# Layer 0's cross-attention: turning the tokens of groups 1 to 3 through DRAM and VectorE instead of on TensorE

## The chip, the cores and the metric

The kernel runs on one core of one Trainium2 chip. The metric is the device time of one execution, in microseconds; the time of a kernel is the median of several runs. A profile is one further execution, recorded by the hardware profiler. Its span runs from the first instruction to the last; the execution's own time is a little longer.

## The reference, cut to what matters

Two decoder layers work on x, 16 blocks of 128 tokens with 512 features, in float32. Each layer has a self-attention, a cross-attention and a feed-forward part, and each part ends in `x = layernorm(x + part(x))`. The change lies in the first layer's cross-attention:

```python
q_hk = (hidden_q @ Wq.T).reshape(b, s, H, K)
q_big = jnp.einsum('bshk,hkq->bshq', q_hk, w_kc_q)
kv_rope = kv_c * cos[None] + _rotate_half(kv_c) * sin[None]
q_r = jnp.einsum('bshq,hqr->bhsr', q_big, W_qr)
k_r = jnp.einsum('bld,hdr->bhlr', kv_rope, W_kr)
attn = jax.nn.softmax(jnp.einsum('bhsr,bhlr->bhsl', q_r, k_r), axis=-1)
ctx_c = jnp.einsum('bhsl,bld->bhsd', attn, kv_rope)
out = jnp.einsum('bhsd,hkd->bshk', ctx_c, w_kc_kv).reshape(b, s, H * K) @ Wo.T
```

There are 16 heads, 128 context rows of 128 features for each block, and 64 features in a head's scores. Every block attends only to its own context, so the 16 blocks are independent.

## The kernel before, in words

**The stage.** The weights are folded earlier: `wqr` (512 x 1024) takes x straight to all heads' queries, `wkr` takes the rotated context to the keys, and `mT[h]` takes a head's context mean to the output. The 16 blocks go in four groups of four (`NG`, `GB`). For a group, `context` (L572 to L581) puts the features of its contexts and tokens on the partitions, since TensorE contracts over partitions: four transposes of the rotated contexts `kvr` against an identity into one PSUM bank `pk` (L575), a ScalarE copy to `kvT` (L577), and for each block `transpose_x` (L123 to L129): four 128x128 transposes into a bank `tr` (L128) and a ScalarE copy into `xT` (L129).

**Two halves.** A group's heads go in two halves of eight. `project(half)` (L583) runs, for each of four column blocks, the matmuls `pq` (L590) and `pk2` (L593) and the copies to `qT` (ScalarE, L591) and `kT` (VectorE, L594). Then four steps follow, one for each block. The 32 steps of the stage are numbered m = 0 to 31, and a step is written (half, i) below, i being the block in its group.

**One step.** `Heads` makes eight scores on TensorE (L607, two PSUM banks `sc`), the negated maximum on VectorE (L214), eight exponentials with their sums on ScalarE (L219), the reciprocal on VectorE (L225) and the scaling on GpSimd (L226). `turn` transposes the probabilities by way of DRAM: VectorE turns 32x32 blocks into `sq` (L624), SyncE's queue writes `sq` to `away` (L628), and four loads from `away` bring it back as `pT` (L631). One step later `values` multiplies with the context (`av`, L637, copied to `cc` at L642), and one more step later `out` applies `mT` (`po`, L649), VectorE adds it to x (L654), and after the second half `layernorm` follows (VectorE and GpSimd, L111 to L122).

**Work beside it.** Each step from m = 4 on handles two pieces of the feed-forward weights (`pieces`): 24 are summed in absolute value (VectorE, L514), then 16 are cut to three levels (VectorE, L541 and L543); each piece is loaded by SyncE's queue (L508) a step ahead into one of two buffers. `rotate` (L406 to L418) loads a group's contexts into the room `ct` and lets GpSimd compute `kvr` with the room `t2` in four operations. It is traced at step (1, 1) of the group before. Both rooms have one buffer.

**The other way to turn tokens.** `Turn` (L132 to L156) is in the kernel already, for other stages. `send`: ScalarE permutes a block's 512 features into `xp` (L144) and SyncE's queue writes it to DRAM (`turned`, L145). `fetch`: four loads, one for 32 partitions each, in runs of 512 bytes (L151). `back`: one VectorE transpose of 32x32 blocks into `xT` (L154).

**What sets the order.** The framework lays down each engine's queue ahead of time. It takes the instructions that are ready by its own estimate of time, those traced first before the others, and a later one may float ahead when it is ready and its buffer is free. On the chip each queue then runs in that fixed order. `keep_in_program_order` pins an instruction behind the one traced last before it on its engine. A tag with one buffer (`xT`, `kvT`, `ct`, `t2`) is given to the next tile when all users of the one before are done.

Of the kernel before, what the change touches and what calls it, by code (L numbers as in the profile page):

```python
# [12 lines left out]
F32 = mybir.dt.float32  # L13
# [5 lines left out]
P = 128  # L19
NB = 16  # L20
D = 512
KC = D // P
# [24 lines left out]
def decoder_kernel(ctx: ExitStack, tc: tile.TileContext, a: dict, out: bass.AP):  # L47
# [25 lines left out]
    def bank(tag, shape, name):  # L73
        return psum.pool.tile(shape, F32, tag=tag, name=name, bufs=psum.banks[tag])
# [45 lines left out]
    def layernorm(b, engine=nc.vector):  # L120
        mean, rstd = statistics(b)
        engine.tensor_scalar(x[b], x[b], mean, rstd, ALU.subtract, ALU.mult)  # L122

    def transpose_x(xT, b, at):

        tr = bank("mm", [P, KC, P], "tr")
        for k in range(KC):
            nc.tensor.transpose(tr[:, k, :], x[b][:, k * P : (k + 1) * P], ident)  # L128
        nc.scalar.copy(xT[:, :, at : at + P], tr)  # L129
# [159 lines left out]
    GB = 4  # L289
    TG = GB * P  # L290
    NG = NB // GB
# [10 lines left out]
    def fold(pool, i, raw, take):  # L302

        cT = pool.tile([P, P], F32, tag="cT", name="cT")
        ch = pool.tile([P, 2, R], F32, tag="ch", name="ch")

        def inner():
            pc = bank("mm", [P, P], "pc")
            for q in range(3):
                for j in range(2):  # L310
                    nc.tensor.matmul(
                        pc[j * R : (j + 1) * R], lhsT=raw[:, j, D + DCQ + q * R : D + DCQ + (q + 1) * R],
                        rhs=raw[:, j, D + q * P : D + (q + 1) * P], start=(q == 0), stop=(q == 2),
                    )
            nc.vector.tensor_copy(cT, pc)

        def turned():
            pc = bank("mm", [P, P], "pcT")
            nc.tensor.transpose(pc, cT, ident)
            nc.vector.tensor_copy(ch.rearrange("p j r -> p (j r)"), pc)  # L320

        def behind(j):
            o = D + DCQ + 3 * R
            pm = bank("mm", [P, D], "pm")
            nc.tensor.matmul(pm, lhsT=raw[:, j, o : o + DC], rhs=raw[:, j, o + DC : o + DC + D], start=True, stop=True)
            take(mT[2 * i + j], pm)

        def outer():
            pg = bank("mm", [P, KC, 2, R], "pg")
            for k in range(KC):  # L330
                for j in range(2):
                    nc.tensor.matmul(
                        pg[:, k, j, :], lhsT=raw[:, j, k * P : (k + 1) * P], rhs=ch[:, j, :], start=True, stop=True
                    )
            nc.vector.tensor_copy(wqr[:, :, i * P : (i + 1) * P], pg.rearrange("p k j r -> p k (j r)"))

        return [(0.8, inner), (0.86, lambda: behind(0)), (0.2, turned), (0.86, lambda: behind(1)), (1.9, outer)]

    with tc.tile_pool(name="p1", bufs=1) as p1:
# [67 lines left out]
        def rotate(g, ct, kvr, t2):  # L407

            blocks = slice(g * GB, (g + 1) * GB)
            nc.sync.dma_start(ct, a["ctx"][blocks].rearrange("b l d -> l b d"))  # L410

            def turn():
                nc.gpsimd.tensor_tensor(t2[:, :, 0:hd], ct[:, :, hd:DC], bc(s2[:, 0:hd], GB), ALU.mult)
                nc.gpsimd.tensor_tensor(t2[:, :, hd:DC], ct[:, :, 0:hd], bc(s2[:, hd:DC], GB), ALU.mult)
                nc.gpsimd.tensor_tensor(kvr, ct, bc(c2, GB), ALU.mult)
                nc.gpsimd.tensor_tensor(kvr, kvr, t2, ALU.add)

            return turn  # L418
# [128 lines left out]
    with tc.tile_pool(name="p2", bufs=1, reuse_waits="tile") as p2:  # L547
# [8 lines left out]
        def pieces():  # L556

            tern.limits()
            while loaded:
                (n, q, run), raw = loaded.pop(0)  # L560
                run(n, q, raw)
            for _ in range(2):
                if todo:
                    loaded.append((todo[0], tern.load(*todo[0][:2], p2)))
                    todo.pop(0)
# [3 lines left out]
        def room(name):  # L569
            return p2.tile([P, GB, DC], F32, tag=name, name=name)  # L570

        def context(g, kvr):  # L572
            pk = bank("mm", [P, GB, P], "pk")
            for i in range(GB):
                nc.tensor.transpose(pk[:, i, :], kvr[:, i, :], ident)  # L575
            kvT = p2.tile([P, TG], F32, tag="kvT", name="kvT")
            nc.scalar.copy(kvT, pk.rearrange("p b l -> p (b l)"))  # L577
            xT = p2.tile([P, KC, TG], F32, tag="xT", name="xT")
            for i in range(GB):
                transpose_x(xT, g * GB + i, i * P)  # L580
            return xT, kvT  # L581

        def project(xT, kvT, half):  # L583
            qT = p2.tile([P, 4, TG], F32, tag="qT", name="qT")
            kT = p2.tile([P, 4, TG], F32, tag="kT", name="kT")
            for c in range(4):
                cols = slice((4 * half + c) * P, (4 * half + c + 1) * P)
                pq = bank("mm", [P, TG], "pq")
                for k in range(KC):
                    nc.tensor.matmul(pq, lhsT=wqr[:, k, cols], rhs=xT[:, k, :], start=(k == 0), stop=(k == KC - 1))  # L590
                nc.scalar.copy(qT[:, c, :], pq)  # L591
                pk2 = bank("mm", [P, TG], "pk2")
                nc.tensor.matmul(pk2, lhsT=wkr[:, cols], rhs=kvT, start=True, stop=True)  # L593
                nc.vector.tensor_copy(kT[:, c, :], pk2)  # L594
            return qT, kT
# [3 lines left out]
        class Heads:  # L599
# [44 lines left out]
            def out(self, par):  # L644
# [8 lines left out]
                if par == 1:  # L653
                    nc.vector.tensor_tensor(x[self.b], x[self.b], self.po, ALU.add)  # L654
                    if self.half == 1:
                        layernorm(self.b)

        kvr = kvr0
        late = []
        for i in range(LATE, H // 2):  # L660
            raw = pre.tile([P, 2, RAW], F32, tag="pre", name=f"raw{i}")
            nc.sync.dma_start(raw, a["l0x_raw"][i].rearrange("p (h n) -> p h n", h=2))
            late += fold(p2, i, raw, nc.vector.tensor_copy)
        held = {}
        steps = [(g, half, i) for g in range(NG) for half in range(2) for i in range(GB)]
        for m in range(len(steps) + 2):
            if m < len(steps):
                g, half, i = steps[m]
                if i == 0:
                    if half == 0:  # L670
                        kv, (xT, kvT) = kvr, context(g, kvr)
                    qT, kT = project(xT, kvT, half)
                held[m] = Heads(g * GB + i, half, qT, kT, kv[:, i, :])
                while late:
                    late.pop(0)[1]()
                held[m].turn()
                if (half, i) == (1, 1) and g + 1 < NG:
                    kvr = p2.tile([P, GB, DC], F32, tag="kvr", name="kvr", bufs=2)
                    rotate(g + 1, room("ct"), kvr, room("t2"))()
            if m >= 2:  # L680
                held[m - 2].out(0)
            if 1 <= m <= len(steps):
                held[m - 1].values()
            if m >= 2:
                held.pop(m - 2).out(1)
            if m >= 4:
                pieces()
        while todo or loaded:
# [8 lines left out]
    with tc.tile_pool(name="p3", bufs=1) as p3:  # L697
# [34 lines left out]
        for g in range(NG):  # L732
            hs = []
            if g + 1 < NG:
                coming, more = inputs(g + 1)
# [31 lines left out]
            for i in range(GB):  # L767
                b = g * GB + i
# [15 lines left out]
    with tc.tile_pool(name="p4", bufs=1) as p4:  # L784
# [31 lines left out]
        coming = []  # L816
# [7 lines left out]
        for g in range(NG):  # L824
            if g == 0:
                xT = p4.tile([P, KC, TG], F32, tag="xT", name="xT")
# [31 lines left out]
            if g + 1 < NG:  # L858
                xT = p4.tile([P, KC, TG], F32, tag="xT", name="xT")
# [167 lines left out]
    with tc.tile_pool(name="p6", bufs=1, reuse_waits="tile") as p6:  # L1027
# [16 lines left out]
        xTs = []  # L1044
# [4 lines left out]
        with tc.tile_pool(name="p6a", bufs=1, side="right", reuse_waits="tile") as p6a:  # L1049
# [22 lines left out]
            def gt(name, shape=(P, NB, E)):  # L1072
                return p6a.tile(list(shape), F32, tag=name, name=name)
# [3 lines left out]
            m = gt("gm", (P, NB))  # L1077
# [64 lines left out]
            first = gt("first", (P, E + 1))  # L1142
# [394 lines left out]
```

## Time and profile before

| what | value |
|---|---|
| runs | 2071.18, 2070.22, 2071.78 us; median 2071.18 |
| the profiled execution's own time | 2073.39 us |
| its span | 2071.6 us |
| granted TensorE clock, mean | 0.992 |

The stage lies between about 255 and 757 us of the span. By stretch, from the view of busy time by window:

| stretch, us | content | PE busy | DVE | ACT | POOL | DMA share |
|---|---|---|---|---|---|---|
| 255 to 324 | group 0, half 0, and the start | 64.81 | 21.86 | 20.42 | 20.56 | 0.33 |
| 324 to 382 | group 0, half 1 | 57.99 | 22.34 | 18.18 | 9.11 | 0.24 |
| 382 to 441 | group 1, half 0 | 57.84 | 26.52 | 20.63 | 10.64 | 0.38 |
| 441 to 499 | group 1, half 1 | 57.99 | 24.50 | 18.66 | 8.82 | 0.39 |
| 499 to 560 | group 2, half 0 | 59.85 | 29.23 | 21.41 | 12.61 | 0.36 |
| 560 to 618 | group 2, half 1 | 57.99 | 30.18 | 18.66 | 9.27 | 0.40 |
| 618 to 680 | group 3, half 0 | 61.09 | 28.08 | 21.88 | 12.20 | 0.28 |
| 680 to 757 | group 3, half 1, and the end | 75.18 | 24.88 | 23.33 | 11.43 | 0.22 |

How to read it: PE is TensorE, DVE VectorE, ACT ScalarE, POOL GpSimd, and SPq the queue of SyncE, which issues nearly all transfers. Busy times are microseconds within the stretch. In the views below a line begins with start and duration in microseconds; "xT<-tr" means that xT is written from tr; and "[1.16 <-ACT xT L129]" means that the engine sat idle for 1.16 us just before, until ScalarE's instruction of line 129 was done. "x8" is a number of instructions merged into the line.

### The profile page before, as it was taken

The numbers are of one execution on the slowest core, as the hardware profiler recorded it, in microseconds if no ns is written. First come the engines' busy times: TensorE is split into PE (matmuls) and PEld (weight loads), VectorE is DVE, ScalarE is ACT, GpSimd is POOL, SyncE is SP. The second block draws the span as 40 slices with busy tenths as digits, with TensorE's granted clock in tenths as the row PEclk, the third lists the DMA queues.
The fourth block names the chain that finished last, engine by engine and source line by source line (L and its number), as shares of the span: only waits on it lengthen the run. The fifth ranks groups of instructions, "written<-read, shape, count | busy, mean of one in ns | idle before, by whom it ended". The sixth has DMA issues, their size and how long they took to land.

```text
span 2071.6 us, 25330 instructions
## 1 busy us (share of the span) xinstructions
PE 2014.1 (97%) x9093; PEld 1115.7 (54%) x9093; DVE 878.6 (42%) x1763; ACT 627.6 (30%) x2107; POOL 646.8 (31%) x674
## 2 busy tenths in 40 slices
PE   8999999999999999999999999999899999999997
PEld 4555554444444458888554445555544455555552
DVE  4777732444554254432134314777731122232234
ACT  3555532333333333222310112766622200000002
POOL 6445530111211113233322113455613222223223
PEclk9999989999999999999999999999999999999999
DMA  9201231344432232001310018500023256786844
GB/s 249 78 25 40 104 124 52 104 127 137 132 117 83 66 118 71 21 11 54 143 51 22 11 34 266 204 22 21 27 66 118 87 141 178 226 237 188 247 108 168
DMA packets 155470, 221.58 MB, mean 107 GB/s; under 512 B 49616, under 2 KB 110416, under 8 KB 150608
## 3 DMA queue, kind: packets, MB, share of 16 engines
q1 hardware_dynamic: 140448, 146.51, 22.6%
q0 software_dynamic: 13792, 72.14, 11.6%
q8 instruction: 72, 1.18, 0.2%
q10 hardware_dynamic: 1104, 1.31, 0.2%
q14 instruction: 54, 0.44, 0.1%
HBM read 182.73 MB, written 72.69 MB: 123 GB/s over the span
## 4 chain that ended last, share of the span: by engine, by line
PE 85%; DMA 5%; DVE 4%; POOL 3%; ACT 2%; issue 1%; SPq 0%; POOLq 0%; DVEq 0%; ACTq 0%
PE po L649 10%; PE po L176 7%; PE pq L590 5%; PE pq L841 5%; PE pq L165 5%; PE pg L1116 4%; PE ry L1265 4%; PE po L772 4%; PE pa L745 4%; PE pb L745 4%; DMA ew<-in_l1f_w_dram,which 4%; PE rg L1244 4%; PE ru L1244 4%; PE pu L1116 3%; PE pv L851 3%; PE av L637 3%
## 5 line engine op out<-in xcount | busy, mean ns | idle before, releaser
L226 POOL TENSOR_TENSOR p<-p,rs 128x512 f32<-128x512 f32 x192 | 200.0, 1043 | 504.0 <-DVE rs L225 494.7
L649 PE MATMUL po<-mT,cc 128*128 128x512 f32 x512 | 231.5, 600 | 0.2 <-ACT cc L642 0.2
L219 ACT ACTIVATE p<-t,nmx 128x128 f32<-128x128 f32 x512 | 198.6, 390 | 34.0 <-POOL p L226 10.2
L649 PEld LDWEIGHTS po<-mT,cc 128*128 128x128 f32 x512 | 95.1, 190 | 114.3 <-issue 106.3
L219 ACT ACTIVATE p<-sc,nmx 128x128 f32<-128x128 f32 x256 | 90.2, 374 | 117.8 <-DVE nmx L214 110.4
L590 PE MATMUL pq<-xT,wqr 128*128 128x512 f32 x256 | 115.7, 593 | 2.9 <-ACT xT L129 2.9
L1214 POOL DMA_INDIRECT ew<-in_l1f_w_dram,which x39 | 40.6, 1042 | 249.1 <-PE ry L1265 182.8
L176 PE MATMUL po<-wo,oT 128*128 128x512 f32 x256 | 116.9, 600 | 0.4 <-ACT qkT L454 0.4
L1249 ACT ACTIVATE rsg<-rg 128x352 f32<-128x352 f32 x39 | 18.1, 464 | 326.4 <-PE rg L1244 310.1
L115 POOL TENSOR_SCALAR ve<-mv 128x1 f32<-128x1 f32 x80 | 18.1, 226 | 303.0 <-DVE mv L113 289.1
L1244 PE MATMUL rg<-ew,xsT 128*128 128x352 f32 x312 | 101.8, 469 | 10.4 <-DMA ew<-in_l1f_w_dram,which 9.6
L841 PE MATMUL pq<-xT,wq 128*128 128x512 f32 x256 | 110.6, 592 | 0.7 <-ACT xT L129 0.7
L1265 PE MATMUL ry<-ew,ractT 128*128 128x512 f32 (+1 forms) x234 | 106.9, 592 | 0.0
L122 POOL TENSOR_SCALAR x<-x,mv,rstd 128x512 f32<-128x512 f32 x48 | 100.5, 2094 | 4.5
L1244 PE MATMUL ru<-ew,xsT 128*128 128x352 f32 x312 | 98.7, 459 | 0.0
L219 ACT ACTIVATION_READ_ACCUMULATOR p<-t,nmx 128x1 f32 x512 | 96.1, 188 | 0.0
L233 DVE COPY pT<-pt 128x512 f32<-128x512 f32 x128 | 86.6, 679 | 19.4 <-PE pt L231 19.4
L756 POOL TENSOR_TENSOR hl<-ht,hh 128x512 fp32r<-128x512 f32 x44 | 57.4, 1306 | 108.2 <-ACT hh L754 108.2
L231 PEld LDWEIGHTS pt<-ident,p 128*128 128x128 f32 x512 | 60.0, 141 | 55.7 <-issue 41.5
L1116 PE MATMUL pg<-xT,sw_gu 128*128 128x512 f32 x192 | 86.5, 593 | 0.0
L1277 POOL DMA_INDIRECT sums<-ry,place x39 | 61.8, 1585 | 74.7 <-DMA sums<-ry,place 37.8
L1251 DVE TENSOR_TENSOR ract<-rsg,ru 128x352 f32<-128x352 f32 x39 | 20.3, 521 | 151.0 <-issue 140.4
(243 smaller groups left out, 3676.4 us busy)
## 6 DMA issues: line engine op xcount, KB each, us to landing
piece<-in_l0f_w_dram SPq DMA_DIRECT2D x48, 352.0 KB
away<-sq SPq DMA_DIRECT2D x32, 512.0 KB
pT<-away SPq DMA_DIRECT2D x128, 128.0 KB
raw<-in_l0x_raw_dram SPq DMA_DIRECT2D x8, 1728.0 KB
slots_x<-zero SPq DMA_DIRECT2D x1, 10023.0 KB
sums<-zero SPq DMA_DIRECT2D x1, 9984.0 KB
xs<-slots_x SPq DMA_DIRECT2D x156, 64.0 KB
x<-turned SPq DMA_DIRECT2D x128, 64.0 KB
```

The source lines that it names most:

```text
L122: engine.tensor_scalar(x[b], x[b], mean, rstd, ALU.subtract, ALU.mult)
L165: nc.tensor.matmul(got["p"], lhsT=lhsT, rhs=rhs, start=(n == 0), stop=(n == len(pairs) - 1))
L176: nc.tensor.matmul(po, lhsT=oT[:, c, :], rhs=wo[:, c, :], start=(c == 0), stop=(c == KC - 1))
L219: nc.scalar.activation(self.p[:, j, :], src[:, j, :], AF.Exp, bias=nmx[:, j : j + 1], accum_out=self.sm[:, j : j + 1])
L226: nc.gpsimd.tensor_tensor(self.p, self.p, spread(rs, P), ALU.mult)
L590: nc.tensor.matmul(pq, lhsT=wqr[:, k, cols], rhs=xT[:, k, :], start=(k == 0), stop=(k == KC - 1))
L649: nc.tensor.matmul(self.po, lhsT=self.cc[:, 4 * par + j, :], rhs=mT[h], start=(par == 0 and j == 0), stop=(par == 1 and j == 3),)
L745: nc.tensor.matmul(dst, lhsT=wt[:, k, f * P : (f + 1) * P], rhs=xs[n][:, k, :], start=(k == 0 and n == 0), stop=(k == KC - 1 and n == 1),)
L841: nc.tensor.matmul(pq, lhsT=wq4[k // 2][:, k % 2, c * P : (c + 1) * P], rhs=xT[:, k, :], start=(k == 0), stop=(k == KC - 1))
L1116: nc.tensor.matmul(dst, lhsT=sw_gu[:, k, at : at + P], rhs=xTs[g][:, k, :], start=(k == 0), stop=(k == KC - 1),)
L1244: nc.tensor.matmul(dst, lhsT=self.xT[:, k, :], rhs=gu[:, k, off : off + FE], start=(k == 0), stop=(k == KC - 1),)
L1265: nc.tensor.matmul(po, lhsT=self.actT[:mw, m_, :], rhs=dn[:mw, m_, :], start=(m_ == 0), stop=(m_ == 2))
```

## The change

`context` turns only group 0's tokens on TensorE. For groups 1 to 3 a new function `beside(g, half, i)`, called after the step's `turn`, uses `Turn` while the group before is at work. With "first" for the next group's first block:

- (0, 0) and (0, 1): `send` of blocks first and first+1, then of first+2 and first+3. The tiles `xp` are put in the rooms `ct` and `t2`.
- (0, 2): `rotate` for the next group, three steps earlier than before, in the same rooms.
- (0, 3): `fetch` of the first two blocks, again into `ct` and `t2`.
- (1, 1): a new `xT` is taken, `back` of these two blocks, then `fetch` of the other two.
- (1, 2): `back` of the other two.
- (1, 3): at the end of the step `context(g + 1)`, which for these groups holds only the four transposes of `kvr` and the copy to `kvT`.

```diff
-            xT = p2.tile([P, KC, TG], F32, tag="xT", name="xT")
-            for i in range(GB):
-                transpose_x(xT, g * GB + i, i * P)
-            return xT, kvT
+            if g == 0:
+                for i in range(GB):
+                    transpose_x(xTs[0], i, i * P)
+            return xTs[0], kvT
...
+        xTs = [p2.tile([P, KC, TG], F32, tag="xT", name="xT")]
+        ROOMS = ("ct", "t2")
+        coming = {}
+
+        def beside(g, half, i):
+            first = (g + 1) * GB
+            if half == 0 and i < 2:
+                for n in range(2):
+                    b = first + 2 * i + n
+                    coming[b] = Turn(b)
+                    coming[b].send(p2, ROOMS[n])
+            if half == 1 and 1 <= i < 3:
+                if i == 1:
+                    xTs[0] = p2.tile([P, KC, TG], F32, tag="xT", name="xT")
+                for n in range(2 * i - 2, 2 * i):
+                    coming.pop(first + n).back(xTs[0][:, :, n * P : (n + 1) * P])
+            if (half, i) in ((0, 3), (1, 1)):
+                for n in range(2):
+                    coming[first + 2 * half + n].fetch(p2, ROOMS[n])
...
-                        kv, (xT, kvT) = kvr, context(g, kvr)
+                        kv, (xT, kvT) = kvr, next_context or context(0, kvr)
...
-                if (half, i) == (1, 1) and g + 1 < NG:
+                if g + 1 < NG:
+                    beside(g, half, i)
+                if (half, i) == (0, 2) and g + 1 < NG:
                     kvr = p2.tile([P, GB, DC], F32, tag="kvr", name="kvr", bufs=2)
                     rotate(g + 1, room("ct"), kvr, room("t2"))()
...
+            if m < len(steps) and steps[m][1:] == (1, 3) and g + 1 < NG:
+                next_context = context(g + 1, kvr)
```

More of the change, by code (lines that the diff above doesn't have):

```diff
@@ L663, in decoder_kernel @@
             late += fold(p2, i, raw, nc.vector.tensor_copy)
+        next_context = None
         held = {}
```

## The prediction

> **What bounds the kernel now.** I read the page first: which engine is full, and which carries the chain that ended last.
>
> ```profile
> PE 2014.1 (97%) x9093; PEld 1115.7 (54%) x9093; DVE 878.6 (42%) x1763; ACT 627.6 (30%) x2107; POOL 646.8 (31%) x674
> PE 85%; DMA 5%; DVE 4%; POOL 3%; ACT 2%; issue 1%; SPq 0%; POOLq 0%; DVEq 0%; ACTq 0%
> ```
>
> TensorE is busy for 97% of the span and carries 85% of the chain. In the changed stage it is tighter still: in the windows by stage it is busy for 57.99 of 58 us in each second half. So what leaves TensorE's queue there shortens the kernel, and what is added elsewhere costs only where TensorE comes to wait for it. Second, I read the timeline of TensorE at the three places where a group begins.
>
> ```profile
> 381.89 0.38 PE L575 MATMUL pk<-ident,kvr 128*128 128x128 f32 x2
> 382.11 1.91 PE L128 MATMUL tr<-ident,x 128*128 128x128 f32 x16
> 385.18 3.70 PE L590 MATMUL pq<-xT,wqr 128*128 128x512 f32 x8 [1.16 <-ACT xT L129]
> ...
> 499.31 1.04 PE L128 MATMUL tr<-ident,x 128*128 128x128 f32 x8
> 500.65 0.77 PE L128 MATMUL tr<-ident,x 128*128 128x128 f32 x5 [0.31 <-DVE x L654]
> 501.25 1.88 PE L637 MATMUL av<-pT,kvr 128*128 128x512 f32 x4
> 502.97 0.49 PE L128 MATMUL tr<-ident,x 128*128 128x128 f32 x3
> 504.30 3.70 PE L590 MATMUL pq<-xT,wqr 128*128 128x512 f32 x8 [0.83 <-ACT xT L129]
> ...
> 618.31 1.04 PE L128 MATMUL tr<-ident,x 128*128 128x128 f32 x8
> 620.25 1.09 PE L128 MATMUL tr<-ident,x 128*128 128x128 f32 x8 [0.90 <-DVE x L654]
> 621.18 1.88 PE L637 MATMUL av<-pT,kvr 128*128 128x512 f32 x4
> ```
>
> The reader is to see two things in each place: the 16 transposes themselves, and the holes around them. TensorE waits for ScalarE's copy of the last transposes (1.16 and 0.83 us) or for a PSUM bank that VectorE has yet to read (0.31 and 0.90 us). At the start of a second half, where nothing is transposed, `pq` follows the step before without a hole.
>
> **What is removed.** Group 1: from 382.11 to 385.18, 3.07 us. Group 2: from 499.31 to 504.30, less the `av` inside (501.25 to 502.97), 4.99 - 1.72 = 3.27 us. Group 3: from 618.31 to 621.18, 2.87 us. Together **9.2 us**: about 5.6 of transposes and 3.6 of holes. The transposes of `kvr` stay; moved to the group's end they cost the same 0.4 us each time, and their copy to `kvT` (0.59 us) is first needed by `pk2`, 3.4 us after the first `pq`. ScalarE loses 12 copies `xT` of 0.60 us.
>
> **What is added, and what covers it.** All four kinds are in the trace, in later stages:
>
> ```profile
> L144 ACT COPY xp<-x x24: 607/619/625, 753.3 to 1058.0; 128x512 f32<-128x512 f32 x24
> L145 SPq DMA_DIRECT2D turned<-xp x24: 319/338/643, 754.2 to 1058.6; - x24
> L151 SPq DMA_DIRECT2D x<-turned x128: 302/430/2053, 40.7 to 1172.3; - x128
> L154 DVE STREAM_TRANSPOSE xT<-x x32: 668/702/711, 88.9 to 1181.2; 128x512 f32<-128x512 f32 x32
> ```
>
> - ScalarE: 12 copies `xp` of 0.62 us against the 12 that go, 0.2 us more in all. It is busy 18 to 22 of some 60 us in a half. For group 1 they float into the first projection (263 to 280 us), where ScalarE has gaps of 3.7 us. Cost between 0 and 1.2: the latter if two of them land between the exponentials at 293 to 300 us, for which TensorE waits there (2.32 and 0.98 us). I take 0, since the rooms are free from 260.87, the first load of `ct`.
> - VectorE: 12 `back` of 0.70 us, two each in the steps (1, 1) and (1, 2). It is busy 7.3 of 10 us at most (608 to 618).
> - SyncE's queue: 12 sends of 0.34 and 48 fetches of 0.43 us, 24.7 us over three groups; a fetch pair is 8 x 0.43 = 3.4 us in one step. A step of about 10 us now has 0.34 + 1.75 + about 1.1 us of issues.
> - Transfers: 12 x 256 KB out and as much in. In the window from 1043 to 1051, which holds fetches of one such pair, 98 GB/s took 0.32 of the engines, so 6.3 MB take about 6.3 / 0.78 x 2.56 = 21 us of all 16 engines, over some 360 us: 0.06 on top of 0.24 to 0.40.
> - GpSimd: `rotate` has the same four operations of 0.73, 0.73, 1.27 and 1.27 us. Those of groups 2 and 3 ran at the very start (from 270 us) as far as buffers allowed; now the rooms are taken by `xp` and `x2` in between, so they run in the steps. One can hold back a scaling `p` (1.04 us) by 1.27 us at most. GpSimd is busy 9 to 13 of 60 us, so I take 0, with 3 x 1.27 as the other end.
>
> **Does the fetch land in time?** The one view that bears on it:
>
> ```profile
> 1043.85 3.64 SPq L151 DMA_DIRECT2D x<-turned  x8
> 1050.22 1.29 DVE L154 STREAM_TRANSPOSE xT<-x 128x512 f32<-128x512 f32 x2
> ```
>
> Eight fetches issued from 1043.85 were used at 1050.22, 6.4 us later, and the listing of L154 shows no idle time of VectorE before any of its 32 transposes. Here the first pair is fetched at (0, 3), two steps and a projection before its `back`. The second pair can only be fetched when the first `back` has freed the rooms, and its own `back` is pinned behind `sq` one step later, about 9.9 us (`away` is issued at 598.53 and 608.40). Budget 9.9 - 1.4 = 8.5 us against 6.4: it fits with 2.1 us to spare.
>
> **What is late next.** The `av` that starts a new group comes earlier by the removed time, but its `pT` does not. Before group 3:
>
> ```profile
> 612.95 0.33 SPq L508 DMA_DIRECT2D piece<-in_l0f_w_dram  x1
> 613.38 1.79 SPq L631 DMA_DIRECT2D pT<-away  x4
> ```
>
> `pT` stands behind a piece's load, and that waits for VectorE to cut the piece before. The four `back` of two steps put 2.8 us of VectorE work ahead of that cut. From the issue of `away` to the first load of `pT` it is 2.72 us where nothing else is between (410.30 to 413.02); I take this as the landing time. Then the last load, issued at 614.7, lands at 614.7 + 2.8 + 2.7 = 620.2, and `av` is due at 618.3: 1.9 us of waiting. Before group 2 the same sum gives 494.85 + 2.8 + 2.72 = 500.4 against 499.3: 1.1 us. Before group 1 it gives 380.2 against 380.17: nothing. The bounds are 3.0 us and 0, the latter if the framework lets TensorE begin with `pq`, of which 17 us are ready and which needs no `pT`. Both orders occur in the trace (`av` ahead of `pq` at 621.18, `pq` ahead of `av` at 560.34), so I take the middle, **1.5 us**.
>
> **The sum.** For the profiled execution, 2073.39 - 9.2 + 1.5 = 2065.7 us. It lies 2.2 us above the median of the runs, so against the median it is 2071.18 - 9.2 + 1.5 = **2063.5 us**, 0.37% less. Differences within 0.2% (4.1 us: 2067.0 to 2075.3) are about what a measurement here cannot tell from no change.
>
> **Rivals.**
>
> - *The gain is eaten by late probabilities.* In the two fetch steps of each group, all eight fetches (3.4 us) go ahead of `pT`. In a middle step `pT`'s last load is issued at 602.5, lands at 605.2, and `av` starts at 607.90: 2.7 us of slack. Each of six steps then loses 0.8 us, 4.7 in all; with the 3.0 above, 7.7. Time 2071.18 - 9.2 + 7.7 = 2069.7. For it: SyncE's queue is in order, and 512 KB of fetch share the engines with `away`, `pT` and pieces at a DMA share of about 0.5 in these steps. Against it: SyncE waits 2.7 us for `away` anyway, and most fetches fit in there.
> - *Slower: VectorE stands at `back`.* If the fetch of the second pair is queued behind the pieces of the next step, or lands as late as that, `back` waits for about a step, and all maxima, reciprocals and `sq` behind it wait too. A whole step of 9.9 us, less the slack of 2.7, in each of three groups is 21.7 us: 2071.18 - 9.2 + 21.7 = 2083.7. It decides from the point where x2 comes more than 2.7 + 3.1 = 5.8 us late in each group. Against it speak the spare 2.1 us and the 32 transposes that never waited; for it, that here the fetch has one step, in a queue that also waits for VectorE.
>
> The Trainium skill has a rule that would bring this about ("VectorE: DVE Perf Modes", section "The three transpose paths"): a plain copy that transposes through strides of its access pattern is 19 times slower than a transposing DMA when the innermost destination stride is large, so 128x128 belongs on TensorE. By that rule the time would lie at or beyond the 2083.7 of this rival. This trace does not agree for these fetches, which keep runs of 512 bytes: 6.4 us from the first issue to use. I hold it at 1 in 100, within this rival.
>
> - *More than the sum.* If everything added is hidden and the earlier chain also shortens a hole at the start, by one of 0.98 us, the time is 2061.0 or less.
>
> **How the numbers follow.** Forecast (2061 to 2067) 0.69; eaten 0.16; slower 0.11; more 0.04. Faster by over 0.2%: 0.69 + 0.04 = 0.73; within: 0.16; slower: 0.11. The range runs from 2060.8, all hidden and a little more, to 2070.0, which takes in the eaten case's 2069.7 and all costs at their upper ends short of it; the slower case and the top of the eaten one stay outside.
>
> **What will show it.** Right: no L128 after 262 us; `pq` of groups 1 to 3 without idle time before it; twelve L154 in the stage with no idle VectorE before them; the stage about 7.7 us shorter, later stages as long as before. Wrong: TensorE idle before `av` until "DMA pT<-away" beyond some 3 us (eaten); VectorE idle until "DMA x<-turned", with ScalarE's exponentials late behind it (slower); a longer wait of `sc` near 295 us for ScalarE (copies at the start). The forecast fails above all if the framework's estimate of landing times is off, so that a fixed queue waits at its head.

## The result, and the profile after

The changed kernel takes 2062.16 us (median of 7 runs, 2057.32 to 2065.75); the kernel before, on the same chip, 2070.22 us (7 runs). The ratio is 0.9958, with a 95% interval from 0.9945 to 0.9972: 0.42% faster, 1.3 us below the forecast. Repeated later with five rounds it was 0.9957 (0.9944 to 0.9971).

The page of the profiled execution (span 2057.5 us), its busy times and the shares of its chain:

```profile
PE 2006.5 (98%) x9045; PEld 1110.9 (54%) x9045; DVE 886.6 (43%) x1775; ACT 627.7 (31%) x2107; POOL 647.5 (31%) x674
PE 84%; DMA 6%; DVE 3%; POOL 2%; issue 2%; ACT 1%; SPq 0%; POOLq 0%; DVEq 0%; ACTq 0%
```

TensorE has 48 instructions fewer (12 blocks x 4 transposes), VectorE 12 more, and the bound is the same. The two profiled executions differ by 2073.39 - 2059.38 = 14.0 us. Only 9.3 of that is the stage: from the first transpose of `kvr` to the first `tr` of the feed-forward part it fell from 494.2 to 484.9 us. The rest lies outside, where nothing was changed; a second profile of the kernel before gave 2065.95 us with a stage of 493.6, one of the changed kernel a stage of 485.4. So the stage repeats to 0.6 us while the whole scatters by several, and I read the experiments by the stage.

The timeline of TensorE at the three places where a group begins (start, duration):

```profile
377.66 0.60 PE L575 MATMUL pk<-ident,kvr 128*128 128x128 f32 x4
378.10 3.60 PE L590 MATMUL pq<-xT,wqr 128*128 128x512 f32 x8
...
383.25 1.88 PE L637 MATMUL av<-pT,kvr 128*128 128x512 f32 x4
...
493.19 0.60 PE L575 MATMUL pk<-ident,kvr 128*128 128x128 f32 x4
493.63 3.60 PE L590 MATMUL pq<-xT,wqr 128*128 128x512 f32 x8
...
499.64 1.88 PE L637 MATMUL av<-pT,kvr 128*128 128x512 f32 x4
...
610.05 0.60 PE L575 MATMUL pk<-ident,kvr 128*128 128x128 f32 x4
610.49 3.60 PE L590 MATMUL pq<-xT,wqr 128*128 128x512 f32 x8
...
617.36 1.88 PE L637 MATMUL av<-pT,kvr 128*128 128x512 f32 x4
```

The transposes and the holes are gone; `pq` starts behind `pk` without idle time, and `av` comes 10 to 14 `pq` matmuls later instead of at the head of the group. The added VectorE transposes, listed within the stage, with what they waited for:

```profile
L154 DVE STREAM_TRANSPOSE xT<-x x12: 669/683/714, 357.3 to 605.1; 128x512 f32<-128x512 f32 x12
its engine sat idle before it (us, times) until:
```

In the view no line follows under "sat idle": VectorE never stood at one. (Once, at 481.07, the view names "DMA x<-turned" for a wait of 1.22 us ahead of `sq`. Other waits ahead of `sq` last 1.22 us too and end with GpSimd's scaling, as at 354.77, so I read this one as the same.) SyncE's queue before group 3, where the prediction saw `pT` late:

```profile
609.34 0.33 SPq L508 DMA_DIRECT2D piece<-in_l0f_w_dram  x1
609.77 1.80 SPq L631 DMA_DIRECT2D pT<-away  x4
611.66 0.38 SPq L508 DMA_DIRECT2D piece<-in_l0f_w_dram  x1
```

The issue of the last load of `pT` begins at 611.1. With the 2.72 us of the prediction it lands at 613.9 (an estimate), and `av` needs it at 617.36. Finally TensorE's waits in the stage, for the kernel before and then for the changed one (us in total, times, longest):

```profile
PE sc L607 <- ACT p L219: 3.3, 2, 2.3
PE pq L590 <- ACT xT L129: 2.9, 3, 1.2
PE tr L128 <- DVE x L654: 1.2, 2, 0.9
...
PE po L649 <- ACT cc L642: 0.2, 1, 0.2
```

```profile
PE sc L607 <- ACT p L219: 3.4, 2, 2.3
PE po L649 <- ACT cc L642: 1.4, 1, 1.4
PE pq L590 <- ACT xT L129: 0.9, 1, 0.9
```

The waits at the boundaries are gone (the 0.9 left is group 0's), no wait names `pT`, and one is new: 1.4 us of `po` for `cc`.

### The profile page after: what moved, and what is told of

Same layout as the page of the kernel before. It is cut to its first block, busy times and chain, and to the rows that moved or that the text cites. A ratio compares the mean times of both kernels' runs of the same rounds, so it can differ in the third digit from the quotient of the medians.

```text
span 2057.5 us, 25359 instructions
## 1 busy us (share of the span) xinstructions
PE 2006.5 (98%) x9045; PEld 1110.9 (54%) x9045; DVE 886.6 (43%) x1775; ACT 627.7 (31%) x2107; POOL 647.5 (31%) x674
## 4 chain that ended last, share of the span: by engine, by line
PE 84%; DMA 6%; DVE 3%; POOL 2%; issue 2%; ACT 1%; SPq 0%; POOLq 0%; DVEq 0%; ACTq 0%
PE po L649 10%; PE po L176 7%; PE pq L590 5%; PE pq L868 5%; PE pq L165 5%; PE pg L1143 4%; PE po L799 4%; PE pa L772 4%; PE pb L772 4%; PE pu L1143 3%; DMA sums<-ry,place 3%; PE ry L1292 3%; PE rg L1271 3%; PE ru L1271 3%; PE pv L878 3%; PE av L637 3%
## 5 line engine op out<-in xcount | busy, mean ns | idle before, releaser
L226 POOL TENSOR_TENSOR p<-p,rs 128x512 f32<-128x512 f32 x192 | 201.0, 1048 | 456.9 <-DVE rs L225 447.6
L219 ACT ACTIVATE p<-t,nmx 128x128 f32<-128x128 f32 x512 | 198.6, 390 | 33.8 <-POOL p L226 10.2
L122 POOL TENSOR_SCALAR x<-x,mv,rstd 128x512 f32<-128x512 f32 x48 | 100.5, 2094 | 4.5
L783 POOL TENSOR_TENSOR hl<-ht,hh 128x512 fp32r<-128x512 f32 x44 | 57.4, 1305 | 108.1 <-ACT hh L781 108.1
L1304 POOL DMA_INDIRECT sums<-ry,place x39 | 61.8, 1585 | 70.4 <-DMA sums<-ry,place 34.7
L214 DVE TENSOR_REDUCE nmx<-t 128x4 f32<-128x512 f32 x128 | 83.6, 676 | 0.8
```

The lines of the kernel that those rows point to most:

```text
L219: nc.scalar.activation(self.p[:, j, :], src[:, j, :], AF.Exp, bias=nmx[:, j : j + 1], accum_out=self.sm[:, j : j + 1])
L226: nc.gpsimd.tensor_tensor(self.p, self.p, spread(rs, P), ALU.mult)
```

## The experiments

**How I compare.** Beside the ratio to the kernel before on the same chip I give the stage, and its parts: the time from the first key projection (`pk2`) of each half to that of the next, in us. The last column runs to the stage's end; the 6.8 us ahead of the first are left out. In the changed kernel an `av` (1.72 us) stands behind the first `pk2` of groups 1 to 3 instead of ahead of it, so 1.7 us shift from the column with the arrow to the next one.

| kernel | stage | g0 h0 | h1 → g1 | g1 h0 | h1 → g2 | g2 h0 | h1 → g3 | g3 h0 | end | ratio (95%) |
|---|---|---|---|---|---|---|---|---|---|---|
| before | 494.2 | 61.6 | 60.5 | 57.7 | 61.5 | 57.7 | 60.8 | 57.3 | 70.3 | |
| before again | 493.6 | 61.0 | 60.5 | 57.7 | 61.5 | 57.7 | 60.8 | 57.3 | 70.3 | one run |
| changed | 484.9 | 61.0 | 55.7 | 59.4 | 56.2 | 60.8 | 56.1 | 59.0 | 70.0 | 0.9958 (0.9945-0.9972) |
| changed again | 485.4 | 61.5 | 55.7 | 59.4 | 56.2 | 60.8 | 56.1 | 59.0 | 70.0 | 0.9957 (0.9944-0.9971) |
| 1 contexts alone | 493.7 | 61.1 | 60.5 | 57.7 | 61.5 | 57.7 | 60.8 | 57.3 | 70.3 | 1.0004 (0.9995-1.0014) |
| 2 tokens early, TensorE | 488.5 | 61.6 | 59.0 | 57.7 | 59.1 | 57.7 | 59.0 | 57.3 | 70.3 | 0.9979 (0.9965-0.9993) |
| 3 both ways | 498.5 | 61.0 | 61.0 | 57.7 | 61.7 | 59.1 | 62.2 | 59.0 | 70.0 | 1.0029 (1.0018-1.0039) |
| 4 transposes twice | 498.1 | 61.3 | 61.8 | 57.7 | 62.5 | 57.7 | 62.7 | 57.4 | 70.3 | 1.0022 (1.0013-1.0031) |
| 5 back twice | 485.7 | 61.1 | 55.7 | 59.4 | 56.2 | 60.8 | 56.1 | 59.7 | 70.0 | 0.9949 (0.9934-0.9964) |
| 6 fetch twice | 493.1 | 61.2 | 55.7 | 63.9 | 56.2 | 64.3 | 56.0 | 59.0 | 70.0 | 0.9999 (0.9989-1.0009) |
| 7 first pairs twice | 489.0 | 61.2 | 55.7 | 63.3 | 56.2 | 60.8 | 56.1 | 59.0 | 70.0 | 0.9989 (0.9978-0.9999) |
| 8 rotate in a step | 489.7 | 66.2 | 55.7 | 59.5 | 56.2 | 60.3 | 56.1 | 59.0 | 70.0 | 0.9974 (0.9962-0.9986) |
| 9 one exponential pinned | 483.4 | 61.0 | 55.7 | 59.4 | 56.2 | 59.4 | 56.0 | 59.0 | 70.0 | 0.9944 (0.9932-0.9956) |
| 10 no. 7, pinned | 485.0 | 61.4 | 55.7 | 59.1 | 56.2 | 60.8 | 56.1 | 59.0 | 70.0 | 0.9959 (0.9946-0.9973) |

Put right for the moved `av`, the changed kernel's arrow columns are 57.4, 57.9 and 57.8: 3.2, 3.6 and 3.1 us less than before, 9.8 in all (the prediction's 9.2). Of the columns behind them only g2 h0 is longer, by 1.4 us.

**Theory and rival.** Theory: the time comes from TensorE's queue at the three boundaries, and everything added fits beside it. Rival: the added work does cost, through VectorE, the transfers or GpSimd, and something else pays for it. Two kernels without an edit first, for the scatter.

> The kernel before, unchanged, to see how far one profile differs from the next. The stage is measured from the first transpose of group 0's contexts to the first transpose of the feed-forward part: 494.2 us before, 484.9 us with the change. Every theory expects 494.2 within 0.5 us; a larger difference would mean that stage lengths of single profiles can't be compared to a microsecond.

> The change, unchanged, for a second profile and more pairs of runs. Theory: stage 484.9 within 0.5 us, total 0.4% under the kernel before. Rival (much of the difference of the first profiles lay outside the stage by chance): the stage differs by 9 us again, while the totals differ by less.

Measured: rows 2 and 4 of the table.

**1. The contexts alone.** Groups 1 to 3 keep their TensorE transposes; only `rotate` and the transposes of `kvr` move.

```diff
-            first = (g + 1) * GB
-            ...
+            pass
...
+                        xT = xTs[0] if g == 0 else p2.tile([P, KC, TG], F32, tag="xT", name="xT")
+                        for n in range(GB):
+                            transpose_x(xT, g * GB + n, n * P)
```

> Only the contexts are transposed at the group's end and rotated at (0, 2); the tokens of all groups are transposed on TensorE at the start of their group, as before. Theory (the 16 token transposes per group and the holes around them are the gain): stage 493.5 to 494.5 us, holes before pq of groups 1 to 3 as before, no change of the total. Rival (the gain is the new order of contexts and rotation): stage 487 us or less.

Stage 493.7, as before. The gain is all in the tokens.

**2. The tokens moved, but turned on TensorE.** Each group's transposes stand in the steps (1, 1) and (1, 2) of the group before.

```diff
-                    coming.pop(first + n).back(xTs[0][:, :, n * P : (n + 1) * P])
+                    transpose_x(xTs[0], first + n, n * P)
```

> The tokens of groups 1 to 3 are transposed on TensorE, but in the steps (1, 1) and (1, 2) of the group before, without DRAM and VectorE. Theory (5.6 us of transposes and 3.6 us of holes): only the holes close, stage 494.2 - 3.6 = 490.6 us, at most 491.5. Rival (only the order matters, the transposes themselves hide): 485 us, as with the change. Rival (the holes come back elsewhere): 494 us.

The timeline of TensorE in one such step:

```profile
351.88 1.16 PE L607 MATMUL sc<-kT,qT 64*128 64x128 f32 x16
352.97 1.09 PE L128 MATMUL tr<-ident,x 128*128 128x128 f32 x8
353.90 5.32 PE L649 MATMUL po<-mT,cc 128*128 128x512 f32 x12
```

Eight transposes take 0.93 us to the next start, no less than before, and nothing waits around them. Yet the stage is 488.5, lower than the 490.6 expected. Over groups 1 to 3 (arrow and h0 columns) the move alone closes 1.5, 2.3 and 1.8 us, 5.7 in all. To see where, I add up the time from each TensorE instruction to the start of the next, over these six columns, by what it computes:

| us | transposes of tokens | of it at 0.116 each | idle around them | `sc`, `po`, `av` | `pq` |
|---|---|---|---|---|---|
| before | 9.20 | 5.57 | 3.63 | 240.57 | 82.61 |
| 2 tokens early | 5.57 | 5.57 | 0 | 238.75 | 82.41 |
| changed, with its new hole of 1.4 | 0 | 0 | 0 | 241.59 | 82.41 |
| 9, without that hole | 0 | 0 | 0 | 240.15 | 82.41 |

`pk`, `pk2` and `ptot` are alike in all four. The holes are worth their 3.6 us. The other 2.0 us come from scores, `po`, `av` and `pq`, which stand in another order there and take less time; why is not shown.

**3. Both ways.** Sends and fetches stay, the VectorE transposes turn each block in place, unused, and TensorE turns the tokens at the group's start as well.

```diff
-                    coming.pop(first + n).back(xTs[0][:, :, n * P : (n + 1) * P])
+                    x2 = coming.pop(first + n).x2
+                    tc.keep_in_program_order(nc.vector.transpose(x2, x2))
```

> Everything that the change adds is done (sends, fetches, VectorE's transposes, here in place in the fetched tile, whose result is not used), and the tokens are still transposed on TensorE at the start of their group. Contexts as in the change. Theory (the additions are hidden): stage 494.2 us plus 0 to 1.5. Rival (the additions cost several us and the change gains more than it shows): 497 us or more.

A miss: 498.5. In g2 h0 1.4 us are lost in the hole that the changed kernel has too. Some 3 us are lost at group 3 (in its two columns together, since here too an `av` stands behind the first `pk2`), in the timeline of TensorE and in the granted clock (column after POOL's busy time) of one microsecond behind it:

```profile
618.08 1.04 PE L128 MATMUL tr<-ident,x 128*128 128x128 f32 x8
620.65 1.09 PE L128 MATMUL tr<-ident,x 128*128 128x128 f32 x8 [1.54 <-DVE x L651]
622.47 5.40 PE L587 MATMUL pq<-xT,wqr 128*128 128x512 f32 x8 [0.73 <-ACT xT L129]
```

```profile
623.00:624.00 1.00, 1.00 (x2) 0.34 (x1) 0.96 (x3) 0.00 (x0) 0.00 (x0) 0.50 1.01 407
```

VectorE's update of x came later, so the hole that was 0.90 us is 1.54, and with the 0.73 behind it the clock fell to half: eight `pq` took 5.40 us instead of 3.60. So the additions are not free where TensorE still waits for VectorE; in the changed kernel that wait is gone.

**4. TensorE's transposes twice,** in the kernel before.

```diff
-        for k in range(KC):
-            nc.tensor.transpose(tr[:, k, :], x[b][:, k * P : (k + 1) * P], ident)
+        for _ in range(times):
+            for k in range(KC):
+                nc.tensor.transpose(tr[:, k, :], x[b][:, k * P : (k + 1) * P], ident)
...
-                transpose_x(xT, g * GB + i, i * P)
+                transpose_x(xT, g * GB + i, i * P, 1 if g == 0 else 2)
```

> The kernel before, with the 16 token transposes of groups 1 to 3 done twice, into the same bank. Theory (TensorE's queue is the bound at these places, so each transpose of 0.118 us counts in full): stage 494.2 + 5.6 = 499.8 us. Rival (another chain sets the time there, and transposes only fill its waiting): under 496 us.

Stage 498.1: over groups 1 to 3, 48 more transposes cost 4.3 us, less than 48 x 0.116 = 5.6, since part of them falls into the holes, which shrink from 3.6 to 2.1 us.

**5. The VectorE transposes twice.**

```diff
-                    coming.pop(first + n).back(xTs[0][:, :, n * P : (n + 1) * P])
+                    for _ in range(2):
+                        coming[first + n].back(xTs[0][:, :, n * P : (n + 1) * P])
```

> The change, with each VectorE transpose of the tokens done twice: 12 more of 0.70 us, 8.4 us, all in the steps (1, 1) and (1, 2). Theory (VectorE has room there): stage 485 to 487 us. Rival (VectorE is the next bound of these steps): 8.4 us less the slack of 2.7 us in each group's two steps, some 489 us or more.

Stage 485.7, with VectorE busy 219.1 instead of 210.9 us in it. VectorE has room for 8.2 us more, but not quite for nothing: g3 h0 is 0.7 us longer, where TensorE now waits for VectorE.

```profile
615.91 1.98 PE L590 MATMUL pq<-xT,wqr 128*128 128x512 f32 x4 [0.42 <-DVE x L654]
```

In the changed kernel, with `back` done once, no such wait stands there.

**6. and 7. The fetches twice.** Behind each pair's fetch the same rows are read once more, into DRAM; in 7 only for the first pair of each group.

```diff
+                for n in range(2):
+                    b = first + 2 * half + n
+                    rows = turned[b].rearrange("(t r) (q f) -> q r t f", r=QP, q=4)
+                    for q in range(4):
+                        tc.keep_in_program_order(nc.sync.dma_start(spare[b, q], rows[q]))
```

> The change, and behind each pair's fetches the same eight reads once more, into a spare tensor in DRAM, in the same queue. Stage with the change: 484.9 us. Theory (SyncE's queue and the transfers have room in these steps): 485 to 486.5 us. Rival (they have none, late probabilities eat the gain): each of six steps loses up to 3.4 us more, 490 us or more, with TensorE idle until pT lands.

The expectation failed: 493.1, with 4.5 us lost in g1 h0 and 3.5 in g2 h0. But no wait names `pT`. The timelines of GpSimd and VectorE in group 1:

```profile
409.91 0.73 POOL L413 TENSOR_TENSOR t<-ct,s 128x256 f32<-128x256 f32 x1 [4.93 <-DMA ct<-in_ctx_dram]
...
412.52 0.22 POOL L115 TENSOR_SCALAR ve<-mv 128x1 f32<-128x1 f32 x1
412.82 0.57 POOL L117 TENSOR_TENSOR rstd<-ve,nhalf 128x1 f32<-128x1 f32 x1
413.35 1.26 POOL L416 TENSOR_TENSOR kvr<-kvr,t 128x512 f32<-128x512 f32 x1
```

```profile
413.42 1.48 DVE L122 TENSOR_SCALAR x<-x,mv,rstd 128x512 f32<-128x512 f32 x1 [2.96 <-POOL rstd L117]
...
416.41 0.67 DVE L214 TENSOR_REDUCE nmx<-sc 128x4 f32<-128x512 f32 x1
```

The sends took until 404.5, so the contexts were loaded at 406.2 instead of 393.6, and `rotate`, which in the changed kernel is done at 400.6, stands ahead of the layernorm's `rstd` in GpSimd's queue. VectorE waits 2.96 us for it, the maxima `nmx` come 4.4 us later than in the changed kernel (412.01; the half itself began 0.9 us later here), and at 428 TensorE waits 1.12 and 0.91 us for exponentials.

> The change, with the doubled reads behind the first pair's fetch at (0, 3) only, so that the sends and rotate of the next group aren't held back. Theory (GpSimd's place, not the room in queue and transfers): stage 485 to 486.5 us, rotate of groups 2 and 3 in the projection as with the change. Rival (the added reads themselves delay the probabilities): half of the 8 us that the full doubling cost, 488 to 490 us.

Here `rotate` stayed where it was and g2 lost nothing, but g1 lost 3.9 us. First TensorE, then ScalarE in the same step, then the granted clock of one microsecond behind the hole:

```profile
427.55 1.96 PE L637 MATMUL av<-pT,kvr 128*128 128x512 f32 x4 [0.17 <-issue]
431.82 8.83 PE L649 MATMUL po<-mT,cc 128*128 128x512 f32 x16 [2.31 <-ACT cc L642]
```

```profile
430.48 0.37 ACT L219 ACTIVATE p<-sc,nmx 128x128 f32<-128x128 f32 x1 [4.66 <-DVE nmx L214]
...
430.84 0.36 ACT L219 ACTIVATE p<-sc,nmx 128x128 f32<-128x128 f32 x1
...
431.18 0.58 ACT L642 COPY cc<-av 128x512 f32<-128x512 f32 x1
```

```profile
433.00:434.00 1.00, 1.00 (x3) 0.48 (x2) 0.17 (x1) 1.00 (x7) 0.75 (x1) 0.50 0.70 226
```

`av` ran on time, so `pT` was there. But ScalarE's queue has two exponentials of the next step ahead of the copy that empties `av`, and they wait for maxima. The hole is 2.31 us; behind it the clock is at half for 3.4 us, and sixteen `po` take 8.83 us instead of 7.13. The changed kernel's own 1.37 us at 545.76 looks alike, with one exponential. This is a new theory, a queue's order and no lack of room, and the last two runs test it.

**8. `rotate` pinned into step (0, 1).** It asks what `rotate` costs in GpSimd's queue where it can't slide.

```diff
-                if (half, i) == (0, 2) and g + 1 < NG:
+                if (half, i) == (0, 1) and g + 1 < NG:
...
+                hold(nc.gpsimd.tensor_tensor(kvr, ct, bc(c2, GB), ALU.mult))
```

> The change, with rotate traced at (0, 1) instead of (0, 2) and its four GpSimd operations pinned behind that step's scalings, so that they run inside the step and not in the projection before it. No transfer is added. Theory (in the kernel with doubled fetches it was GpSimd that lost the time: rotate, 4 us, stood ahead of the layernorm's rstd, VectorE waited for it, and TensorE for the scores' banks): the first halves of groups 1 and 2 grow by 2 to 5 us each, as there, stage 489 to 494 us. Rival (it was the added transfers): stage 485 to 486.5 us.

The size fits, the place does not: the theory foresaw the loss in groups 1 and 2, and they lost nothing. There `rotate` came behind the step's `rstd` and scalings, and the next `rstd` hardly waited (VectorE stood 1.08 us for it in group 1, 0.94 in the changed kernel). Group 0 lost 5 us, at its start, where TensorE waits for the softmax anyway:

```profile
303.75 0.71 DVE L624 STREAM_TRANSPOSE sq<-p 128x512 f32<-128x512 f32 x1 [4.05 <-POOL p L226]
```

```profile
299.54 3.47 PE L607 MATMUL sc<-kT,qT 64*128 64x128 f32 x16 [1.82 <-DVE sq L624]
...
309.03 9.74 PE L649 MATMUL po<-mT,cc 128*128 128x512 f32 x16 [2.31 <-ACT cc L642]
```

The four operations (3.9 us) hold back the scalings, VectorE's transposes and so TensorE: its waits there add up to 3.3 us more than in the changed kernel, and the clock is at half for 17.1 instead of 10.2 us.

**9. and 10. One exponential pinned.** In both, one exponential is pinned behind the copies `cc`: in 9 on top of the change, for step (0, 3) of group 2 (m = 19); in 10 on top of no. 7, for step (0, 3) of group 1 (m = 11). All other queues keep their instructions and their order.

```diff
+                if pin and j == 0:
+                    tc.keep_in_program_order(exp)
...
-                held[m] = Heads(g * GB + i, half, qT, kT, kv[:, i, :])
+                held[m] = Heads(g * GB + i, half, qT, kT, kv[:, i, :], m == 19)
```

> The change, with the first exponential of step (0, 3) of group 2 pinned behind the copies cc of the step (0, 1). The instructions and the order of every other queue are those of the change; on ScalarE one exponential moves behind two copies. In the change TensorE waits there 1.37 us for cc before po. Theory (the hole is made by ScalarE's queue order alone): the hole goes, group 2's first half falls from 60.8 to about 59.4, the stage from 484.9 and 485.4 to 483.5 to 484.2, the time by about 1.4 us. Rival (ScalarE or VectorE has no room there, and the hole only moves): po no longer waits, but the scores or av of the next step do; the stage stays at 484.7 or more.

ScalarE and TensorE at that place, in the changed kernel and with the pin (two lines more in the file, so `cc` is L644 and `po` L651):

```profile
544.77 0.37 ACT L219 ACTIVATE p<-sc,nmx 128x128 f32<-128x128 f32 x1 [3.86 <-DVE nmx L214]
...
545.13 0.57 ACT L642 COPY cc<-av 128x512 f32<-128x512 f32 x1
```

```profile
545.76 7.13 PE L649 MATMUL po<-mT,cc 128*128 128x512 f32 x16 [1.37 <-ACT cc L642]
```

```profile
543.15 0.59 ACT L644 COPY cc<-av 128x512 f32<-128x512 f32 x1 [2.29 <-PE av L639]
```

```profile
544.26 7.13 PE L651 MATMUL po<-mT,cc 128*128 128x512 f32 x16
```

The copy starts 2 us earlier, the hole is gone, g2 h0 is 59.4 instead of 60.8 and the stage 483.4. The theory held. At 0.9944 this is the fastest of all the kernels; its interval overlaps the changed kernel's, so the 1.4 us are shown by the stage and the hole, not by the times.

> The kernel that reads the first pairs twice, with the first exponential of step (0, 3) of group 1 pinned behind the copies cc. Both reads stay, and so does every other queue; on ScalarE two exponentials move behind the copies. Theory (the 3.8 us lost in group 1's first half came from these two exponentials ahead of cc, and the low granted clock from the hole that they made): that half falls from 63.2 to 59.4 to 60.0, the stage from 489.0 to 485 to 486, and the granted clock there is 0.95 or more. Rival (the added transfers themselves delay what TensorE needs there, or lower the clock): the half stays at 62 or more, the stage at 488 or more, with the wait at another instruction or the clock low without a hole.

```profile
428.25 1.95 PE L639 MATMUL av<-pT,kvr 128*128 128x512 f32 x4 [0.19 <-DMA pT<-away]
430.08 7.13 PE L651 MATMUL po<-mT,cc 128*128 128x512 f32 x16
```

The theory held here too: g1 h0 is 59.1, the stage 485.0, the clock 1.00, although all the added reads are there (227 GB/s from 432 to 436 us). What no. 7 lost was lost by the order of two instructions and the clock behind the hole, not by the transfers. In no. 6 I did not pin `rotate` behind `rstd`; that its whole loss has that cause is read from the trace only.

## Why the prediction was right, point by point

- **The bound: right.** What left TensorE's queue shortened the kernel; the doubled VectorE transposes (5) cost 0.7 us at one place, against 8.2 us of work.
- **Removed, 9.2 us: right, and its split too; 9.8 measured.** The table of experiment 2 gives the 48 transposes and the holes 9.20 us before, 5.57 and 3.63, as I had read them. Both are gone. The 0.6 us more are in `sc`, `po` and `av` together (0.4) and in `pq` (0.2), which my sum held fixed. That the move alone (2) closes 5.7 us and taking the transposes away only another 4.2 does not make them cheaper: in 2 the other matmuls take 2.0 us less, in the changed kernel only 0.6.
- **Additions hidden: right, with one of them mis-sized.** VectorE and transfers: no wait of TensorE names them. ScalarE's copies at the start: nothing that stands out of the scatter (the waits at 294 and 298 us are 2.32 and 1.08, in the second profile 2.32 and 1.78, against 2.32 and 0.98, in the second profile 2.31 and 0.78; the first column is 61.0 and 61.5 against 61.6 and 61.0). `rotate` cost 0 because in group 1 it fell into the projection (396.6 to 400.6), not into the steps as I wrote; in group 2 its last two operations ran in a step (519.6 to 522.2), without harm. Pinned into a step it cost nothing (8, groups 1 and 2) or 5 us (8, group 0), so the end of the range that I gave, 1.27 a time, was too small.
- **"What is late next", 1.5 us for `pT`: right in the delay, wrong in who waits, and near the size by luck.** The loads did come later, as foreseen: against the group's first `pk` the last one is issued 3.4, 3.2 and 4.2 us later than before. But no TensorE wait names `pT`, since the queue begins with `pq`, the case that I gave for the lower bound. Had `av` come first, the last load plus 2.72 us (378.5, 495.1 and 613.9, against 378.1, 493.6 and 610.5) would by the same estimate have cost 0.4, 1.4 and 3.4, 5.2 in all and so more than my upper bound of 3.0. In its place 1.4 us are lost at 545.76, to ScalarE's order, which I did not look at (9 shows it).
- **The sum:** -9.2 + 1.5 = -7.7, measured -9.8 + 1.4 = -8.4 in groups 1 to 3 and -8.2 to -9.3 in the stage, from four profiles. The larger error, 0.6, is in the first term.
- **The signs.** In the stage no L128 comes after group 0's, `pq` of groups 1 to 3 starts without idle time and the twelve L154 without a wait, as written. "Later stages as long as before" can't be told: outside the stage the two profiles differ by 4.7 us, and runs of the kernel before alone by 5 (2067.79 to 2072.85).
- **The rivals.** *Eaten by late probabilities* did not happen, nor when the fetches were doubled: there the stage did lose its gain, but by the traces through GpSimd's and ScalarE's queues. *VectorE stands at `back`* did not happen in any run with these transposes (at most 0.2 us of idle time before them in all, where they are done twice). The rule of the Trainium skill that I weighed ("VectorE: DVE Perf Modes", section "The three transpose paths") does not reach this case: the twelve transposes by DRAM never waited. *More than the sum* did not happen either: the first wait at group 0's start is as long as before.

## What to carry to other kernels

In a stage that TensorE fills, work costs its own time and the holes around it, here 5.6 and 3.6 us, and the timeline shows both, from one start to the next. Moving the work to a place without holes already gives the second part. When something is added beside a full engine, free time on the other engines says little; read in each in-order queue what the new instruction, or one that it pushes, comes to stand ahead of. Where a copy that empties a PSUM bank stands behind an exponential that waits for another engine, one pinned instruction can give the time back.

## What the runs showed of the hardware

**A hole can cost more than its length.** In every profile here the changes of the granted clock lie whole multiples of 3.41 us apart, and a dip to 0.50 lasts one such step or several. Holes with a dip behind them: 2.31 us (no. 7), 1.54 and 0.73 (no. 3), 1.12 and 0.91 us (no. 6). Each dip lasted 3.4 us, in which TensorE did about half of its work: 1.7 us more in no. 7 (8.83 against 7.13) and 1.8 in no. 3. Holes without one: 1.37 us (545.76, changed kernel), and in no. 6 also 1.53 and 0.92 us, 2.45 together within 2.9 us:

```profile
548.46 0.48 PE L607 MATMUL sc<-kT,qT 64*128 64x128 f32 x2 [1.53 <-ACT p L219]
549.86 0.94 PE L607 MATMUL sc<-kT,qT 64*128 64x128 f32 x12 [0.92 <-ACT p L219]
```

```profile
545.00:557.00 12.00, 8.02 (x31) 3.73 (x30) 9.49 (x17) 6.21 (x31) 2.08 (x2) 1.00 0.59 166
```

So the sum of the idle times does not decide. Where they fall against the steps may: counted within one step they are 2.3, 2.0 and 1.8 us in the three with a dip, 1.4 and 1.5 in the two without. But ahead of the dip at the stage's start (294.43, kernel before) the step holds only 1.4 us of this hole, and no run tests it. The Trainium skill ("TensorE: Matmul & The Clock Gate", section "What's actually happening") has the clock halved after an idle window of about 3.4 us. The length of the dips agrees with such a window, but here TensorE was never idle for so long.

**VectorE and GpSimd slow each other down.** In no. 6 VectorE's L122 took 1.48 us, begun 0.07 us after GpSimd's L416 of 1.26 us; in the changed kernel it takes 0.55. The Trainium skill ("SBUF — State Buffer", section "Who interferes with whom") describes a pair of ports that one of the two holds for a whole instruction while the other is blocked. The trace agrees as far as it goes: L122 ends 0.3 us after L416, as if it had done most of its work only then. GpSimd's L416, which came first, took 1.26 us as in the changed kernel. The other way round, GpSimd's scaling (L226, 1.04 us otherwise) took 1.72 us in the changed kernel at 609.97, where VectorE's L543 had begun at 609.84.
